# A two-layer graph-attention kernel: two PSUM banks of the first layer's tables serve the output products and the back-transposes once the tables are made

## The chip, the cores and the metric

The kernel runs on one core of a Trainium2 chip. The metric is the device time of one execution in microseconds (us). Three runs of the kernel before gave 2523.47, 2530.24 and 2531.26 us; the median, 2530.24, is the time to compare with. One further execution was taken with the hardware profiler; all traces here are of such an execution.

The names of the engines are those of the profile: PE is the matrix engine (PEld its weight loads), DVE the vector engine, ACT the scalar engine, POOL the engine that here mostly issues indirect DMAs, SP the engine that issues plain DMAs.

## The reference, cut to what matters

The input x has 8 batches of 2048 nodes with 256 features; adj is a sparse symmetric 0/1 matrix of 2048 x 2048, some 9 neighbours a node.

```python
def layer0(x):                               # 4 heads of 64
    q, k, v = x @ Wq.T + bq, x @ Wk.T + bk, x @ Wv.T + bv
    s = clip(q k^T / 8, -10, 10); s = where(adj == 0, -10, s)
    attn = softmax of s inside each chunk of 256 keys   # 8 softmaxes for a row
    out = x + (sum over the chunks of attn v) @ Wo.T + bo
    return layernorm(x + layernorm(out) * gamma + beta)
def layer1(x):                               # 4 heads of 64
    Wh = x @ W;  e = leaky_relu(Wh_i a_src + Wh_j a_dst), only where adj != 0
    return layernorm(x + elu(softmax(e) Wh))
```

The kernel doesn't compute the dense matrices. Each node has a list of its neighbours, and rows of keys and values are fetched by these lists.

## The kernel before

**Tiles and lists.** `edge_lists` makes neighbour lists and sorts the nodes by their number of neighbours, so that a tile of 128 nodes t needs a known number of slots, CAPS[t] (24 for tile 0, 5 for tile 15, 164 in all 16 tiles). Batches go in groups: layer 0 works on G = 2 batches at a time (4 groups g of 16 tiles, so 64 steps i = 0 to 63), layer 1 on 4 batches at a time (2 groups p of 16 tiles, so 32 steps).

**A step of layer 0.** `fetch0` gathers, with one indirect DMA a slot on POOL (line L489), rows of the table `kv_d[g]` into buffers `u`, two slots each; there are 14 of these buffers in a ring. `scores0` forms the scores on DVE (L547, L554) and PE (L566, L576), `softmax0` the weights, and `context0` weighs the gathered rows on DVE (L501) and ACT (L507) and sums them on PE into a bank `acc` (L514); ACT copies the sum out as `cT` (L626). Only when L514 has read a buffer `u` can POOL gather into it again. One step later `finish0` multiplies `cT` by Wo into a PSUM bank (L635, with the bias by L313), DVE reads that bank twice (L641), and then come the two layernorms on ACT and DVE (L451 to L470, L645, L647), whose result is `o`. Two steps later `rows1` transposes `o` (L307, ACT copy L658) and multiplies it by W, batch by batch, into a PSUM bank each (L663, copied out by L664 to L666); SP stores the rows into layer 1's table `wh_d` (L667).

**The tables.** While group g is worked on, `tables` makes the tables of group g + 1, one tile a step, in two banks named `tk` (`chunk_x` L336, keys and values L372 and L376, queries L385, and two small products in a group's last tile). The tables of the last group, 3, are finished in step 47.

**A step of layer 1.** `fetch1` gathers rows of `wh_d[p]` in the same ring; `softmax1` (L680 to L700) forms the weights, `context1` weighs and sums (L501, L507, L514) into two banks `acc`, which ACT copies out as two tiles `hT` (L722), and SP loads the residual `xr` (L725). One step later `finish1` transposes each `hT` back into a PSUM bank (L734), ACT takes the exponential from it (L737), DVE the maximum (L738), and then come L741, the layernorm, and, later still, scatters of the result on POOL (L748, L753).

**The eight PSUM banks** are two `acc`, two `tf`, one `pr`, two `tk` and one `mf`. In the loop, `mf` is used by `rows1` (two times a step of layer 0), `finish0` (once) and `finish1` (two times a step of layer 1); every use waits until the one before has been read out.

**The order.** `seq` lists the steps: 32 of layer 0, then two of layer 0 and one of layer 1 by turns, three steps of layer 1, and 16 of layer 1 alone. In one pass of the loop the calls stand in this order: scores0, the softmax1 of the next layer-1 step, finish1 and context1 of the one that waits, rows1(i-2), finish0(i-1), tables, softmax0, context0. That order is what a compiler reads: it places buffers, sets the semaphores and fixes each engine's own order of instructions, which isn't quite that of the text; on the chip each engine follows that order and waits where it must.

Of the kernel before, what the change touches and what calls it, by code (L numbers as in the profile page):

```python
# [36 lines left out]
G = 2  # L37
# [136 lines left out]
def sparse_path(ctx: ExitStack, tc: tile.TileContext, keep, x, adj, Wq, bq, Wk, bk, Wv, bv, Wo, bo, gamma, beta, W, a,  # L174
# [6 lines left out]
    NG = B // G  # L181
# [50 lines left out]
    def bank(tag, bufs=2):  # L232

        return ps.tile([P, 512], F32, tag=tag, name=tag, bufs=bufs)
# [75 lines left out]
    def add_bias(dst, bias):  # L310

        for c in range(KC):
            nc.tensor.matmul(dst[:, c * P:(c + 1) * P], bias[:, c:c + 1].to_broadcast([P, P]), ident,  # L313
                             is_transpose=True, start=False, stop=c == KC - 1, skip_group_check=True)
# [132 lines left out]
    def spread(src, sums, n):  # L447


        nm = small.tile([P, n], F32, tag=f"nm{n}", name="nm")  # L450
        nc.scalar.mul(nm, sums, -1.0 / F)  # L451
        m2 = small.tile([P, n], F32, tag=f"m2{n}", name="m2")
        for k in range(n):
            sq = small.tile([P, F], BF16, tag="sq", name="sq", bufs=1)
            nc.scalar.activation(sq, src[:, k, :], AF.Square, bias=nm[:, k:k + 1], accum_out=m2[:, k:k + 1])  # L455
        y = small.tile([P, n], F32, tag=f"y{n}", name="y")
        nc.scalar.activation(y, m2, AF.Ln, scale=1.0 / F, bias=eps)
        nc.scalar.activation(y, y, AF.Exp, scale=-0.5)
        r = small.tile([P, n], F32, tag=f"r{n}", name="r")
        nc.vector.scalar_tensor_tensor(r, m2, F * EPS, y, op0=ALU.add, op1=ALU.mult)  # L460
        nc.vector.scalar_tensor_tensor(r, r, -0.5 / F, y, op0=ALU.mult, op1=ALU.mult)
        nc.vector.scalar_tensor_tensor(r, r, 1.5, y, op0=ALU.add, op1=ALU.mult)
        return nm, r

    def normalized(dst, src, sums, n):

        nm, rs = spread(src, sums, n)
        nc.vector.tensor_tensor(nm, nm, rs, op=ALU.mult)
        for k in range(n):
            nc.scalar.activation(dst[:, k, :], src[:, k, :], AF.Identity, scale=rs[:, k:k + 1], bias=nm[:, k:k + 1])  # L470
# [44 lines left out]
                                 start=first and k == 0 and c == 0, stop=last and k == n - 1, skip_group_check=True)  # L515


    got0, st0 = {}, {}

    late = []  # L520
# [108 lines left out]
    def finish0(g, t):  # L629
        cT = st0.pop((g, t))  # L630
        xb = got0.pop((g, t))[0][:, GF:].rearrange("p (b f) -> p b f", b=G)
        po = bank("mf", 1).rearrange("p (b f) -> p b f", b=G)
        for b in range(G):
            for kc in range(KC):
                nc.tensor.matmul(po[:, b, :], cT[:, b * KC + kc, :], wo[:, kc, :], start=(b == 0 and kc == 0),  # L635
                                 stop=False, skip_group_check=True)
            add_bias(po[:, b, :], biasO[g][:, b])
        o = work.tile([P, G, F], F32, tag="o", name="o")
        sums = small.tile([P, 2, G], F32, tag="sums", name="sums")
        for b in range(G):  # L640
            nc.vector.tensor_tensor_reduce(out=o[:, b, :], in0=po[:, b, :], in1=xb[:, b, :], scale=1.0, scalar=0.0,  # L641
                                           op0=ALU.add, op1=ALU.add, accum_out=sums[:, 0, b:b + 1])
        nm, rs = spread(o, sums[:, 0], G)
        for b in range(G):
            nc.vector.scalar_tensor_tensor(o[:, b, :], o[:, b, :], nm[:, b:b + 1], gamma_r, op0=ALU.add, op1=ALU.mult)  # L645
        for b in range(G):
            nc.vector.scalar_tensor_tensor(o[:, b, :], o[:, b, :], rs[:, b:b + 1], xb[:, b, :], op0=ALU.mult, op1=ALU.add,  # L647
                                           accum_out=sums[:, 1, b:b + 1])
        normalized(o, o, sums[:, 1], G)
        nc.sync.dma_start(x1_d[g // 2][t * P:(t + 1) * P, g % 2, :].rearrange("p (b f) -> p b f", b=G), o)  # L650
        st0[g, t] = o
# [76 lines left out]
    def finish1(p, t):  # L728
        hTs, xr = st1.pop((p, t))
        sums = small.tile([P, 2 * G], F32, tag="sums1", name="sums1")  # L730
        for k, hT in enumerate(hTs):
            ph = bank("mf", 1)
            for c in range(G * KC):
                nc.tensor.transpose(ph[:, c * P:(c + 1) * P], hT[:, c, :], ident)  # L734

            ex = hT.rearrange("p c r -> p (c r)")
            nc.scalar.activation(ex, ph, AF.Exp)  # L737
            nc.vector.scalar_tensor_tensor(xr[:, k], ph, 0.0, xr[:, k], op0=ALU.max, op1=ALU.add)  # L738
            for b in range(G):
                xb, c = xr[:, k, b * F:(b + 1) * F], k * G + b  # L740
                nc.vector.scalar_tensor_tensor(xb, ex[:, b * F:(b + 1) * F], 1.0, xb, op0=ALU.min, op1=ALU.add,  # L741
                                               accum_out=sums[:, c:c + 1])
        yv = xr.rearrange("p k (b f) -> p (k b) f", f=F)
        normalized(yv, yv, sums, 2 * G)

        def scatter():
            if p < NG // 2 - 1:
                nc.gpsimd.indirect_dma_start(  # L748
                    out=hold_v[p][t], out_offset=bass.IndirectOffsetOnAxis(ap=node[:, t:t + 1], axis=0),
                    in_=xr.rearrange("p k f -> p (k f)"), in_offset=None)  # L750
                return
            for b in range(p * 2 * G, (p + 1) * 2 * G):
                nc.gpsimd.indirect_dma_start(  # L753
                    out=out_v[t * B + b],
                    out_offset=bass.IndirectOffsetOnAxis(ap=nodeb[:, t, b - p * 2 * G:b - p * 2 * G + 1], axis=0),
                    in_=yv[:, b - p * 2 * G, :], in_offset=None)
        late.append(scatter)
# [23 lines left out]
    def release(p, t):  # L781


        b0, rows = p * 2 * G, slice(t * P, (t + 1) * P)
        tc.keep_in_program_order(nc.sync.dma_start(
            out_v[NT * B + t * B + b0].rearrange("(b n) f -> n b f", b=B)[rows, b0:b0 + 2 * G, :],
            hold_d[p][rows, :].rearrange("n (b f) -> n b f", f=F)))

    def scatters():
        for f in late:  # L790
            f()
        late.clear()

    def at(i):
        return i // NT, order[i % NT]

    def at1(i):
        return i // NT, order[i % NT] if i >= NT else order1[i]
# [3 lines left out]
    def fetch(k):  # L802

        while fetched[0] <= min(k, len(seq) - 1):
            layer, i = seq[fetched[0]]
            (fetch1(*at1(i)) if layer else fetch0(*at(i)))
            fetched[0] += 1
# [3 lines left out]
    for k, (layer, i) in enumerate(seq):  # L811
        g, t = at1(i) if layer else at(i)
        between = layer == 0 and seq[k + 1][0] == 1
        tables_first = layer == 0 and seq[k + 1][0] == 0 and seq[k + 1][1] % NT == 0
        if not tables_first:
            fetch(k + 1)
        scatters()
        if layer == 0:
            scores0(g, t)
            if between and i + 1 < NG * NT:  # L820
                softmax1(*at1(seq[k + 1][1]))
            if waiting is not None:

                if waiting:
                    finish1(*at1(waiting - 1))
                context1(*at1(waiting))
                waiting = None
            if i > 1:
                rows1(*at(i - 2))
            if i:  # L830
                finish0(*at(i - 1))
            if g + 1 < NG:
                tables(g + 1, i % NT)
            if tables_first:
                fetch(k + 1)
            softmax0(g, t)
            context0(g, t)
        elif seq[k - 1][0] == 0 and seq[k - 1][1] + 1 < NG * NT:
            waiting = i
        else:  # L840

            last = seq[k - 1] == (0, NG * NT - 1)
            if last:
                rows1(*at(NG * NT - 2))
                finish0(*at(NG * NT - 1))
            softmax1(g, t)
            if last:
                rows1(*at(NG * NT - 1))
            finish1(*at1(i - 1))
            context1(g, t)  # L850
            if i >= NT + 2:
                release(g - 1, i - NT - 2)
    scatters()
    finish1(*at1(NG // 2 * NT - 1))
    scatters()
    for t in range(NT - 2, NT):
# [430 lines left out]
```

## Time and profile before

| what | value |
|---|---|
| median of three runs | 2530.24 us (2523.47 to 2531.26) |
| the profiled execution's own time | 2397.55 us |
| its span, first to last instruction | 2395.8 us |
| mean TensorE clock granted | 0.885 of full speed |
| PE, busy | 1900.4 us, 79% |
| PE weight loads, busy | 1622.0 us, 68% |
| DVE, busy | 1833.5 us, 77% |
| ACT, busy | 1409.0 us, 59% |
| POOL, busy | 1505.0 us, 63% |
| DMA, moved | 669.10 MB, mean 279 GB/s |
| L635 `finish0` products | 512 instructions, median 379 ns |
| L663 `rows1` products | 512 instructions, median 386 ns |
| L734 `finish1` transposes | 256 instructions, median 273 ns |

The shares are means over stages that differ. The last instruction that writes a `tk` bank starts at 1429.5 us; layer 0's last `finish0` products start at 1969.9 us; from there on only layer 1 runs. The profiled execution is 132.7 us shorter than the median of the timed runs.

### The profile page before, as it was taken

What the parts mean: (1) busy time and instruction counts of PE and PEld (TensorE: products, weight loads), DVE (VectorE), ACT (ScalarE), POOL (GpSimd) and SP (SyncE); (2) the same over time, 40 slices, a digit from 0 to 9 for tenths busy, and PEclk for the clock granted to TensorE, in tenths of its full rate; (3) what the DMA queues carried; (4) which work ended last, traced back from release to release, by engine and by line L of the source; (5) the groups of instructions that cost most, each with busy time, mean ns of one, the idle gap of its engine ahead of it and who ended that gap; (6) DMA issues with size and microseconds to landing.
All of it is one profiled execution on the core that took longest, in us unless ns stands there. A gap on an engine that the chain in (4) does not pass through costs nothing. (4 is left out here: it accounts for less than half of the span.)

```text
span 2395.8 us, 38844 instructions
## 1 busy us (share of the span) xinstructions
PE 1900.4 (79%) x11946; PEld 1622.0 (68%) x11946; DVE 1833.5 (77%) x4099; ACT 1409.0 (59%) x5036; POOL 1505.0 (63%) x1230
## 2 busy tenths in 40 slices
PE   7686889889899898999988885888678786664764
PEld 5565677778778787777876774776566675554653
DVE  6864587877588988588988886887788887775775
ACT  4573455546566555655565665664356677665766
POOL 3125455672666676376668856774677685787883
PEclk9897899899999999999998997987878987877887
DMA  7737877795889798598879977896679896786884
GB/s 259 242 137 272 265 270 281 260 346 209 316 287 320 260 334 319 212 388 298 302 258 353 360 281 238 285 321 221 230 274 326 306 319 248 278 310 231 302 296 154
DMA packets 239982, 669.10 MB, mean 279 GB/s; under 512 B 43688, under 2 KB 70059, under 8 KB 237719
## 3 DMA queue, kind: packets, MB, share of 16 engines
q0 software_dynamic: 156800, 505.01, 60.1%
q1 hardware_dynamic: 79248, 151.55, 17.2%
q10 hardware_dynamic: 3718, 9.97, 1.3%
q8 instruction: 98, 1.61, 0.3%
q14 instruction: 118, 0.96, 0.1%
HBM read 612.79 MB, written 126.36 MB: 309 GB/s over the span
## 5 line engine op out<-in xcount | busy, mean ns | idle before, releaser
L489 POOL DMA_INDIRECT u<-kv_d,idx x656 | 810.2, 1235 | 436.4 <-PE acc L514 185.7
L514 PE MATMUL acc<-ident,u 128*128 128x128 f32 x5248 | 713.4, 291 | 157.0 <-DVE u L501 89.0
L514 PEld LDWEIGHTS acc<-ident,u 128*128 128x128 f32 x5248 | 637.5, 151 | 220.7 <-DVE u L501 133.2
L489 POOL DMA_INDIRECT u<-wh_d,idx x328 | 416.5, 1270 | 148.2 <-issue 76.4
L566 PE MATMUL pr<-ident,u 128*128 128x128 f32 (+1 forms) x1984 | 287.0, 295 | 78.7 <-DVE u L547 77.2
L501 DVE TENSOR_TENSOR u<-u,al 128x1024 f32<-128x1024 f32 x280 | 334.5, 1234 | 1.5
L566 PEld LDWEIGHTS pr<-ident,u 128*128 128x128 f32 (+1 forms) x1984 | 245.4, 151 | 110.8 <-DVE u L547 104.6
L547 DVE TENSOR_TENSOR u<-u,qx 128x1024 f32<-128x1024 f32 (+1 forms) x248 | 302.0, 1218 | 18.3 <-DMA u<-kv_d,idx 15.1
L501 DVE TENSOR_TENSOR u<-u,z 128x1024 f32<-128x1024 f32 x266 | 314.4, 1212 | 0.6
L507 ACT ACTIVATE u<-u,z 128x64 f32<-128x64 f32 x1008 | 262.0, 337 | 25.0 <-DVE z L700 17.1
L507 ACT ACTIVATE u<-u,al 128x64 f32<-128x64 f32 x800 | 209.1, 342 | 23.2 <-DVE al L607 22.3
L663 PE MATMUL mf<-wa,x1T 128*128 128x264 f32 x512 | 167.6, 455 | 23.1 <-ACT x1T L658 14.8
L351 POOL TENSOR_TENSOR xt<-xt,beta_r 128x1024 f32<-128x1024 f32 x32 | 77.1, 2410 | 143.1 <-PE tk L336 126.3
L385 PE MATMUL tk<-wq,xT 128*128 128x256 f32 x512 | 145.2, 397 | 24.4 <-ACT kvs L379 24.4
L451 ACT ACTIVATE nm<-sums 128x2 f32<-128x2 f32 (+1 forms) x160 | 32.4, 202 | 221.3 <-DVE sums L641 122.6
L372 PE MATMUL tk<-wkv,xT 128*128 128x256 f32 x512 | 151.7, 410 | 12.9 <-ACT xC L341 12.6
L635 PE MATMUL mf<-wo,cT 128*128 128x256 f32 x512 | 148.4, 415 | 6.3 <-ACT whs L666 5.3
L376 PE MATMUL tk<-wkv,xC 128*128 128x256 f32 x512 | 144.5, 399 | 0.0
L663 PEld LDWEIGHTS mf<-wa,x1T 128*128 128x128 f32 x512 | 101.7, 218 | 59.7 <-ACT x1T L658 23.6
L455 ACT ACTIVATE sq<-o,nm 128x256 bf16<-128x256 f32 x256 | 129.7, 507 | 5.3
L554 DVE TENSOR_TENSOR u<-u,qx 128x1024 f32<-128x1024 f32 (+1 forms) x96 | 116.0, 1214 | 16.6 <-DMA qx<-qx_d,node 7.1
L590 DVE TENSOR_SCALAR sc<-tf 128x64 f32<-128x64 f32 (+5 forms) x64 | 14.0, 218 | 138.2 <-PE tf L576 138.2
(168 smaller groups left out, 3254.0 us busy)
## 6 DMA issues: line engine op xcount, KB each, us to landing
kv_d<-kvs SPq DMA_DIRECT2D x48, 512.0 KB, 6.0
wh_d<-whs SPq DMA_DIRECT2D x64, 260.0 KB, 5.8
xt<-in_x_dram SPq DMA_DIRECT2D x64, 256.0 KB, 4.8
qx_d<-xt SPq DMA_DIRECT2D x32, 512.0 KB, 4.4
qx_d<-qs SPq DMA_DIRECT2D x64, 256.0 KB, 5.8
x_d<-o SPq DMA_DIRECT2D x64, 256.0 KB, 5.2
xr<-x_d SPq DMA_DIRECT2D x32, 512.0 KB, 4.9
u<-kv_d,idx POOLq DMA_INDIRECT x656, 6.5
```

The lines of the kernel that those rows point to most:

```text
L372: nc.tensor.matmul(pm[:, 0:F], xT[:, b * KC + kc, rows], wkv[:, kc, 0:F], start=(kc == 0), stop=False, skip_group_check=True)
L376: nc.tensor.matmul(pm[:, F:], xC[:, b * KC + kc, rows], wkv[:, kc, F:], start=False, stop=(kc == KC - 1), skip_group_check=True)
L385: nc.tensor.matmul(qb, xT[:, b * KC + kc, rows], wq[:, kc, :], start=(b == 0 and kc == 0), stop=False, skip_group_check=True)
L455: nc.scalar.activation(sq, src[:, k, :], AF.Square, bias=nm[:, k:k + 1], accum_out=m2[:, k:k + 1])
L489: nc.gpsimd.indirect_dma_start(out=u[:, k, 0:width], out_offset=None, in_=table, in_offset=bass.IndirectOffsetOnAxis(ap=idx[:, t, s0 + k:s ...
L501: nc.vector.tensor_tensor(pv, pv, av, op=ALU.mult)
L507: nc.scalar.activation(pe, pe, AF.Copy, scale=al[:, e, s0 + k:s0 + k + 1])
L514: nc.tensor.matmul(acc[:, c, :], part[:, k, c * P:(c + 1) * P], ident, is_transpose=True, start=first and k == 0 and c == 0, stop=last and ...
L547: nc.vector.tensor_tensor(prod.rearrange("p k j (s w) -> p k j s w", w=W8), u[:, :, 0:GF].rearrange("p s (k j w) -> p k j s w", k=UNIT, w=W8),
L566: nc.tensor.matmul(pr[0:n * W8, k, :], prod[:, j // (NJ // UNIT), j % (NJ // UNIT), :], ident, is_transpose=True, start=(j == 0), stop=(j ...
L635: nc.tensor.matmul(po[:, b, :], cT[:, b * KC + kc, :], wo[:, kc, :], start=(b == 0 and kc == 0), stop=False, skip_group_check=True)
L663: nc.tensor.matmul(pw[:, 0:F + 2 * H], xT[:, b * KC + kc, :], wa[:, kc, :], start=(kc == 0), stop=(kc == KC - 1))
```

## The change

After the scores of each step of layer 0, a flag is set to whether the group at work is the last one (g = 3, steps 48 to 63). While it is not set, `finish0` and `finish1` take their bank from `mf`, as before. Once it is set, they take it from the two `tk` banks. `rows1` stays with `mf`. Nothing is added to or taken from what is computed.

```diff
+    made = [False]
+
+    def end_bank():
+        return bank("tk") if made[0] else bank("mf", 1)
...
     def finish0(g, t):
...
-        po = bank("mf", 1).rearrange("p (b f) -> p b f", b=G)
+        po = end_bank().rearrange("p (b f) -> p b f", b=G)
...
     def finish1(p, t):
...
-            ph = bank("mf", 1)
+            ph = end_bank()
...
             scores0(g, t)
+            made[0] = g + 1 == NG
```

The first user of a `tk` bank in its new role is `finish0` of step 47, which is called in step 48. In all, 17 calls of `finish0` (steps 47 to 63) and 28 calls of `finish1` (layer-1 steps 4 to 31; two banks each) change their bank.

## The prediction

> **What bounds the kernel now.** The change acts only after the tables are made, so I read the span by stages first: the busy time of each engine in four stretches. The columns are the stretch, its length, busy us and (instructions) of PE, its weight loads, DVE, ACT and POOL, the TensorE clock, the DMA share and GB/s.
>
> ```profile
> 1000.00:1430.00 430.00, 380.69 (x2518) 326.67 (x2519) 357.68 (x734) 261.57 (x970) 304.80 (x236) 0.96 0.89 325
> 1430.00:1700.00 270.00, 200.35 (x1256) 173.64 (x1255) 203.83 (x458) 153.04 (x562) 180.76 (x146) 0.80 0.79 272
> 1700.00:1990.00 290.00, 219.25 (x1390) 187.37 (x1388) 245.75 (x539) 172.35 (x637) 205.95 (x158) 0.85 0.81 284
> 1990.00:2200.00 210.00, 133.75 (x901) 116.14 (x900) 144.25 (x373) 144.10 (x502) 153.57 (x125) 0.80 0.74 270
> 2200.00:2396.00 196.00, 113.56 (x772) 96.64 (x772) 134.21 (x310) 126.89 (x448) 133.07 (x108) 0.79 0.69 249
> ```
>
> With the tables gone, no engine is full: from 1430 to 1990 DVE works 449.6 of 560 us, PE 419.6, POOL 386.7. But in POOL's timeline two indirect DMAs in a row always stand 0.30 us apart, so its 304 instructions occupy 386.7 + 304 x 0.30 = 478 us, 85% of this stage. From 1990 to 2396 the same sum is 286.6 + 233 x 0.30 = 357 of 406 us, and between 2063 and 2348 I find no gap of POOL above 1.5 us. POOL paces; what can be won is its gaps. Its waits from 1428 to 1990 (who waited, for whom, us in total, times, longest):
>
> ```profile
> POOL u L489 <- issue: 64.2, 186, 7.8
> POOL u L489 <- PE acc L514: 61.6, 27, 14.9
> POOL qx L527 <- DVE o L647: 8.5, 1, 8.5
> ```
>
> The "issue" line is mostly the 0.30 us spacing. The second counts: POOL can't gather because PE hasn't yet summed a buffer (L514). What PE did before its longest case shows in the timeline from 1634 to 1670 (start, us, engine and line; in brackets the idle time before it and what ended it):
>
> ```profile
> 1637.33 0.59 ACT L626 COPY cT<-acc 128x512 f32<-128x512 f32 x1 [2.71 <-PE acc L514]
> ...
> 1641.35 1.39 PE L566 MATMUL pr<-ident,u 128*128 128x128 f32 x8 [4.05 <-DVE u L547]
> ...
> 1646.35 1.09 ACT L470 ACTIVATE o<-o,nm,r 128x256 f32<-128x256 f32 x2 [4.12 <-DVE nm L468]
> ...
> 1654.34 2.13 PE L663 MATMUL mf<-wa,x1T 128*128 128x264 f32 x4 [0.59 <-ACT whs L666]
> ...
> 1657.06 2.07 PE L635 MATMUL mf<-wo,cT 128*128 128x256 f32 x4 [0.59 <-ACT whs L666]
> ...
> 1661.73 0.42 DVE L641 CUSTOM_DVE_ANT_0 o<-mf,qx 128x256 f32<-128x256 f32 x1 [3.82 <-PE mf L313]
> ...
> 1662.65 1.08 PE L734 MATMUL mf<-ident,hT 128*128 128x128 f32 x4 [0.96 <-DVE sums L641]
> ...
> 1663.70 6.51 PE L514 MATMUL acc<-ident,u 128*128 128x128 f32 x48
> ...
> 1665.94 1.79 POOL L489 DMA_INDIRECT u<-kv_d,idx  x1 [14.92 <-PE acc L514]
> ```
>
> finish0's input cT is there at 1637.9, PE is idle for 4.05 us, and mf is free (its last reader, L641 of the step before, ended at 1632.5). Yet L635 comes at 1657.1, behind both L663 of rows1, whose o was made only at 1647.4. It is so in every step of this stage: L635 follows its cT by 10 to 29 us (once 55), always behind the L663 pair, and rows1 stands before finish0 in the text. L734 of finish1(12) runs at 1991.0, 46 us after its hT (1944.3 to 1945.4), also behind rows1. PE itself does leave the text's order (L514 of context1(13) runs at 1957, before the L307 that the text has ahead of it). So I read: **a one-bank tag is handed out in the order of the text**, and a user that is ready waits for one that isn't. That is worse than the short waits between two users.
>
> **What the Trainium skill says.** "Perfetto Trace Analysis", section Optimization Strategy: look for the gaps of the contended engine, and the same gap repeating can mean that there isn't enough SBUF or PSUM for the next tile. POOL's gaps agree. "PSUM — Partial Sum Buffer", section on bank collisions: engines are to be kept apart by bank, so a reader blocks the writer of the next tile; here 0.59 us pass from ACT's reads to the next L663 or L635. "TensorE: Matmul & The Clock Gate", section on HAM oscillation: PE's idle gaps throttle its clock. The trace agrees in kind: four L663 take 1.16 us at 1965.25 and 2.13 us at 1654.34, and the clock is 0.96 in the tables' stage, 0.80 after it. Fewer instructions in a burst ahead of L514 are so worth between 1 and 2 times their fast price.
>
> **The change part by part.** Nothing is added or removed: 17 finish0 (12 PE instructions each) and 28 finish1 move from mf to two tk banks. No DMA and no arithmetic changes, so the edit itself costs nothing; it moves waits.
>
> (a) *finish0, from 1430 to 1970.* L635 and L313 no longer stand behind rows1; with cT there they fit PE's gaps. Then the PE burst in front of L514 is shorter by one finish0: 2.2 us at the fast clock (1947.56 to 1949.99, less what is woven in), 4.2 at the slow one (1657.06 to 1661.7), and 0.6 of waiting. Six long gaps of POOL end right behind such a burst, at 1633, 1666, 1705, 1789, 1867 and 1904 (9.48, 14.92, 7.53, 2.17, 5.01, 5.39 us). Three at the slow clock give 4.8, 6.8 (with L734 and its wait of 0.96) and 2.17 (all there is), three at the fast one 2.9 each: 22.5. The gap of 8.50 at 1741 waits for L647, which is finish0's own end: it goes when finish0 is early. A scatter's gap of 5.73 at 1483 waits for finish1. Together 36.7 us at most. Not all can stay: DVE has 110 us of idle in this stage, 32.0 of them L641 waiting for PE, and what POOL starts sooner meets the ring again. I take a third, **12 us**; bounds 0 and 37.
>
> (b) *The transition.* POOL's first gather of p = 1 needs every row of wh_d, so rows1(63), so finish0(63):
>
> ```profile
> 1951.59 0.56 ACT L626 COPY cT<-acc 128x512 f32<-128x512 f32 x1
> ...
> 1968.75 1.13 PE L635 MATMUL mf<-wo,cT 128*128 128x256 f32 x4
> ...
> 1990.98 1.11 PE L734 MATMUL mf<-ident,hT 128*128 128x128 f32 x4 [0.59 <-ACT whs L666]
> ...
> 1993.79 1.06 POOL L489 DMA_INDIRECT u<-wh_d,idx  x1 [12.39 <-issue]
> ```
>
> L635 could start at 1952.2, 16.6 us sooner. From L641 (1971.2) the chain takes 22.6 us to the gather; begun at about 1955 it ends near 1977, or later if rows1(62), whose o comes at 1963, or DVE's weighting is in the way. POOL has gathers of p = 0 to issue until 1981.4, so the gap of 12.39 us can close wholly. The next gap, 5.63 us at 2001.8, waits for L514 behind four L734 in a row that wait for L663 and for each other; it can close too. Bounds 0 and 18; I take **10**.
>
> (c) *Layer 1 alone.* The second L734 waits for L738 of the first (45.6 us of PE in 12 waits). But POOL is full there, so this is off the path, and I cost it at nothing: POOL's stream of gathers hides it; without that cover it would be some of DVE's 9.7 us of waiting for L737. Three gaps at 2029, 2046 and 2063 (3.17, 3.57, 3.68) wait for finish1 or the engine it shares: bounds 0 and 10.4, I take 2. At the very end L738 (2376.14) needn't wait for a second L734: L738 could follow its fellow at 2374.3, with the L741 behind it: **1 us**.
>
> Sum: 12 + 10 + 2 + 1 = 25 us of the profiled execution's 2397.55 (span 2395.8), so 2372.5. The timed median is 132.7 us above that execution, and no row says where; I carry the difference over unstretched: 2530.24 - 25 = **2505.2**.
>
> **Rivals.** *B, only the short waits go.* The compiler keeps finish0 behind rows1 for another reason than the bank, or POOL's gaps refill from another wait. Then what goes is PE's waiting for mf between users from 1428 to 1990: L635 4.3, L734 7.3 and 3.9, 15.5 us, of which a third on the path: 5 us, **2525**. For it: L514's gap at 1486.8 (14.00 us, for DVE) has nothing to do with mf. Against it: the free bank at 1637.
>
> *C, slower: early work gets in front on DVE.* Each engine's order is fixed beforehand. finish0's DVE block is 2 x 0.42 (L641), 2 x 0.52 (L645), 2 x 0.51 (L647), 6 accumulator reads or so at 0.08 and 6 small ones at 0.16: 4.4 us. Where it is now placed ahead of the products or the weighting that a buffer's release waits for, POOL waits 4.4 us more. From six of 16 steps on (26 us) that eats the gain; at nine (40 us) the kernel is slower by 15: **2545**. For it: DVE is 85% busy from 1700 to 1990. Against it: DVE waits for finish0's bank (32.0 us) now, and layer 1's own stage is POOL's.
>
> **How the numbers follow.** A gets 0.66, B 0.17, C 0.17. A alone reaches from 10 us to the bounds' sum of 66 us, of which I take 55: 2475 to 2520. The range must hold most of B and the near part of C: 2475 to 2540; outside lie the far end of C and a gain beyond 55. A measurement of this kernel tells about 0.3% (7.6 us) from no change. A and a little of B, less the weak end of A, are faster by more: 0.66; same 0.17; slower 0.17.
>
> **What would show it.** Step (a): L635 soon after its cT and often ahead of L307; "DVE o L641 <- PE mf" (under tk) well under 32 us; POOL's waits for L514 from 1428 to 1990 under 50 us. Step (b): POOL's gap before p = 1 under 5 us. Step (c): L734 pairs without a wait for L738, and layer 1 alone about as long as before, some 400 us. I'm wrong if L635 still trails rows1 (B), or if L635 is early and POOL's waits for L514 grow, with DVE's finish0 block ahead of L501 (C).

## The result, and the profile after

The changed kernel took 2553.84 us (median of 20 executions, 2528.09 to 2576.19), the kernel before on the same chip 2536.78 us (20 executions): a ratio of 1.0071, 95% interval 1.0044 to 1.0097. It is slower by 0.7%, where 1% less was forecast. Ratios here leave out executions more than 1.5% above the fastest one of their kernel, and so rest in places on few of them; beside them I give the difference of the means of all executions, with a 95% bound: here +18.2 ± 7.1 us. The profiled execution of the changed kernel took 2541.85 us (span 2540.0, mean TensorE clock 0.864). Lines of the code past 517 have moved by 6: L635 is now L641, L641 is L647, L663 is L669, L734 is L740, L748 is L754.

The stages first, as before (stretch, length, busy us and instructions of PE, PEld, DVE, ACT and POOL, clock, DMA share, GB/s). The first lies in the tables, the next two are layer 0's last group beside layer 1, the last two layer 1 alone:

```profile
1000.00:1500.00 500.00, 412.11 (x2654) 352.69 (x2655) 361.64 (x746) 272.38 (x1009) 286.80 (x232) 0.92 0.77 275
1553.00:1800.00 247.00, 178.20 (x1150) 154.44 (x1150) 191.83 (x445) 146.68 (x545) 156.45 (x130) 0.84 0.76 267
1800.00:2085.00 285.00, 200.26 (x1230) 170.35 (x1230) 211.91 (x452) 138.38 (x510) 178.17 (x142) 0.82 0.71 250
2110.00:2320.00 210.00, 129.27 (x864) 118.38 (x863) 146.26 (x358) 142.09 (x503) 152.50 (x124) 0.77 0.80 292
2320.00:2540.00 220.00, 128.21 (x877) 115.63 (x875) 147.00 (x340) 141.00 (x498) 150.22 (x118) 0.76 0.64 227
```

The tables' stage, which the change doesn't touch, is slower too: DMA moves 275 GB/s there against 325, DVE is busy 72% of it against 83%. So this trace and that of before differ by more than the change, and I keep that for the experiments. POOL's waits while both layers run, 1553 to 2085:

```profile
POOL u L489 <- PE acc L514: 95.1, 22, 13.8
POOL u L489 <- issue: 58.2, 183, 2.5
POOL hold_d L754 <- ACT xr L470: 16.7, 1, 16.7
```

The forecast wanted the first under 50 us (61.6 before). The wait of 8.5 us for the end of finish0 is gone, but a scatter (L754) waits 16.7 us. The transition, where layer 0 ends:

```profile
2084.73 0.59 ACT L632 COPY cT<-acc 128x512 f32<-128x512 f32 x1 [2.98 <-remote]
...
2085.37 1.68 PE L641 MATMUL tk<-wo,cT 128*128 128x256 f32 x4 [2.99 <-issue]
...
2099.27 0.38 DVE L706 TENSOR_TENSOR z<-z,r 128x224 f32<-128x224 f32 x1
2099.69 1.22 DVE L501 TENSOR_TENSOR u<-u,z 128x1024 f32<-128x1024 f32 x1
...
2104.92 1.94 POOL L489 DMA_INDIRECT u<-wh_d,idx  x1 [12.59 <-PE acc L514]
```

L641 starts 0.05 us after cT is done, where L635 took 16.6 us. It is so in all 17 steps: L641 follows cT by 0.05 to 4.4 us, against 9.8 to 54.6 us before. The reading of the bank's order was right. But POOL has a new gap of 12.59 us. DVE did finish0(63)'s and finish1(12)'s L647 to L653, L744 and L747 between 2089.52 and 2099.05, inside softmax1(13)'s chain (L690 at 2090.46, L706 at 2099.27); only then comes the weighting L501 that POOL's next buffer waits for. That is rival C's mechanism, seen here at one place.

### The profile page after: what moved, and what is told of

Its sections match the earlier page's. It is cut to its first block, busy times and chain, and to the rows that moved or that the text cites. A ratio compares the mean times of both kernels' runs of the same rounds, so it can differ in the third digit from the quotient of the medians.

```text
span 2540.0 us, 38839 instructions
## 1 busy us (share of the span) xinstructions
PE 1925.9 (76%) x11946; PEld 1653.5 (65%) x11946; DVE 1829.7 (72%) x4099; ACT 1408.9 (55%) x5036; POOL 1478.5 (58%) x1230
## 4 chain that ended last, share of the span: by engine, by line
PE 28%; DVE 16%; issue 9%; ACT 8%; DMA 5%; another core or an unknown queue 3%; POOL 1%; SPq 0%; POOLq 0%; DVEq 0%; ACTq 0%
PE acc L514 10%; DVE u L501 6%; PE pr L572 4%; PE mf L669 4%; ACT u L507 2%; DVE u L553 2%; DMA u<-wh_d,idx 2%; ACT sq L455 2%; PE mf L641 2%; PE tf L582 2%; DMA u<-kv_d,idx 1%; PE tk L641 1%; PE tk L376 1%; PE tk L385 1%
## 5 line engine op out<-in xcount | busy, mean ns | idle before, releaser
L489 POOL DMA_INDIRECT u<-kv_d,idx x656 | 793.4, 1209 | 551.3 <-PE acc L514 280.1
L514 PE MATMUL acc<-ident,u 128*128 128x128 f32 x5248 | 721.6, 296 | 177.8 <-issue 106.3
L514 PEld LDWEIGHTS acc<-ident,u 128*128 128x128 f32 x5248 | 659.2, 154 | 232.8 <-issue 127.1
L489 POOL DMA_INDIRECT u<-wh_d,idx x328 | 402.3, 1227 | 184.5 <-issue 81.9
L501 DVE TENSOR_TENSOR u<-u,al 128x1024 f32<-128x1024 f32 x280 | 336.9, 1243 | 1.4
L501 DVE TENSOR_TENSOR u<-u,z 128x1024 f32<-128x1024 f32 x266 | 313.2, 1213 | 0.4
L553 DVE TENSOR_TENSOR u<-u,qx 128x1024 f32<-128x1024 f32 (+1 forms) x248 | 296.4, 1195 | 18.4 <-DMA u<-kv_d,idx 16.6
L669 PE MATMUL mf<-wa,x1T 128*128 128x264 f32 x512 | 168.6, 456 | 52.2 <-issue 25.5
L385 PE MATMUL tk<-wq,xT 128*128 128x256 f32 x512 | 157.3, 423 | 46.5 <-ACT kvs L379 39.4
L669 PEld LDWEIGHTS mf<-wa,x1T 128*128 128x128 f32 x512 | 101.0, 217 | 91.7 <-issue 35.6
L385 PEld LDWEIGHTS tk<-wq,xT 128*128 128x128 f32 x512 | 98.3, 213 | 60.8 <-ACT kvs L379 43.7
L372 PEld LDWEIGHTS tk<-wkv,xT 128*128 128x128 f32 x512 | 95.9, 206 | 59.2 <-ACT kvs L379 29.7
L378 ACT COPY kvs<-tk 128x256 f32<-128x256 f32 x128 | 47.5, 371 | 138.2 <-remote 71.3
```

What stands on the lines that cost most here:

```text
L372: nc.tensor.matmul(pm[:, 0:F], xT[:, b * KC + kc, rows], wkv[:, kc, 0:F], start=(kc == 0), stop=False, skip_group_check=True)
L385: nc.tensor.matmul(qb, xT[:, b * KC + kc, rows], wq[:, kc, :], start=(b == 0 and kc == 0), stop=False, skip_group_check=True)
L489: nc.gpsimd.indirect_dma_start(out=u[:, k, 0:width], out_offset=None, in_=table, in_offset=bass.IndirectOffsetOnAxis(ap=idx[:, t, s0 + k:s ...
L501: nc.vector.tensor_tensor(pv, pv, av, op=ALU.mult)
L514: nc.tensor.matmul(acc[:, c, :], part[:, k, c * P:(c + 1) * P], ident, is_transpose=True, start=first and k == 0 and c == 0, stop=last and ...
L553: nc.vector.tensor_tensor(prod.rearrange("p k j (s w) -> p k j s w", w=W8), u[:, :, 0:GF].rearrange("p s (k j w) -> p k j s w", k=UNIT, w=W8),
```

## The experiments

**First, the halves.** The theories were: (1) finish0's early vector-engine blocks stand in front of the weighting (rival C), (2) finish1 and its scatters do, (3) any new order moves the time by some tenths of a per cent. Kernel before on this chip: 2589.27 us.

`control` is the kernel before with blank lines added, the same program.

> The kernel before with seven empty lines, so that its lines carry the numbers of the changed kernel. The same program: ratio 1.000, and its spread says what a ratio is worth. Its trace is the one to compare with. Theory 1 (finish0's early layernorm gets in front of the weighting): POOL's waits for L514 between the end of the tables and the end of layer 0 are near 60 us here, against 107.7 in the changed kernel. Rival 2 (the chip of the first trace was a faster one, and the waits of any kernel are longer on this one): they are near 100 here too.

Measured: 0.9974 (0.9940 to 1.0007), mean +1.7 ± 7.1 us. So large is the uncertainty of one comparison. POOL's wait for L514 from the end of the tables to the end of layer 0 (1608 to 2147):

```profile
POOL u L489 <- PE acc L514: 120.0, 27, 16.6
```

That isn't near 60 us, as in the first trace; it is more than the changed kernel's 95.1. Two more traces that have the old order in this stage and such a chip, `before_shift` and `l1part` (below), show 79.2 and 113.5 us for it. So the rise from 61.6 to 95.1 us isn't the change's: the rival of a quicker chip holds.

`f0only` leaves finish1 on mf:

```diff
-            ph = end_bank()
+            ph = bank("mf", 1)
```

> Only finish0 takes the tk banks, finish1 stays with mf. Theory 1 (finish0 starts 10 to 29 us sooner and its layernorm gets in front of what the sums L514 wait for): the whole loss, ratio 1.007. Rival 2 (finish1's early start does it, its scatters stand in POOL's order ahead of gathers and wait): ratio 1.000. Rival 3 (any new order of instructions gives or takes some tenths of a per cent, whoever is moved): anything from 0.993 to 1.010.

Measured: 1.0003 (0.9973 to 1.0033), mean -0.9 ± 6.3 us.

`f1only` leaves finish0 on mf:

```diff
-        po = end_bank().rearrange("p (b f) -> p b f", b=G)
+        po = bank("mf", 1).rearrange("p (b f) -> p b f", b=G)
```

> Only finish1 takes the tk banks, finish0 stays with mf behind rows1. Theory 1: 1.000 or a little below, 0.998. Rival 2 (finish1's early start does it): 1.007. Rival 3 (any new order): anything from 0.993 to 1.010, and not what the other half leaves over.

Measured: 0.9995 (0.9966 to 1.0024), but mean +8.6 ± 7.2 us.

`onequeue` gives `rows1` the same banks, so that all three stand in one line for two of them:

```diff
-            pw = bank("mf", 1)
+            pw = end_bank()
```

> rows1 takes the tk banks as well once the tables are made, so that all three users share one line of two banks in the order of the text, and finish0 stays behind rows1. The second bank without the overtaking. Theory 1: the loss is gone, ratio 0.995 to 1.000. Rival 2 (finish1): finish1 is behind rows1 as well, so the loss is gone too; the runs with one half tell the two apart. Rival 3: anything from 0.993 to 1.010.

Measured: 0.9993 (0.9963 to 1.0024), mean -4.3 ± 7.4 us. Here L641 stayed 9.8 to 49.1 us behind cT (in the repetition below): the second bank alone does not free finish0, the order of the text does bind. Theory 1 as stated fell: finish0 alone costs nothing that can be measured, though in the trace of `f0only` L641 follows cT by less than 5 us.

**Second, the stages.** Kernel before: 2580.95 us. `both2` is the changed kernel again.

> The change as it is, once more, beside its parts on one chip. Theory 1 (finish0's and finish1's vector-engine blocks, both early now, stand ahead of the softmax and the weighting while layer 0 and layer 1 run by turns): 1.007. Theory 2 (the loss is made where layer 0 ends and in layer 1 alone: the blocks of finish0(63) and finish1(12) inside softmax1(13)'s chain, and finish1's pairs after that): 1.007. Theory 3 (the loss is an offset of a few tenths of a per cent that any new order or any chip gives): anything from 0.998 to 1.004.

Measured: 1.0052 (1.0022 to 1.0082), mean +15.3 ± 7.4 us. The loss is repeated; with the first result +16.8 ± 5.1 us.

`l0part` goes back to mf at each pass of layer 1 alone; `l1part` has `True` in that place, and leaves out the line that sets the flag in layer 0:

```diff
             last = seq[k - 1] == (0, NG * NT - 1)
+            made[0] = False
```

> finish0 and finish1 use the tk banks only while layer 0 runs (steps 48 to 63); finish0(63) and all of layer 1 alone are back on mf. Theory 1: 1.006, and POOL's waits for L514 over 100 us in the stage of both layers as in the changed kernel. Theory 2: 1.000, with the gap of about 12 us before p = 1 back and the first gathers after it without a long wait for L514. Theory 3: 0.997 to 1.004.

Measured: 1.0028 (1.0000 to 1.0055), mean +13.2 ± 8.6 us.

> The tk banks only from the first pass of layer 1 alone: finish0(63) and finish1(12) to finish1(31) on tk, all before on mf. Theory 1: 1.000, with the order of the stage of both layers as before. Theory 2: 1.005, with the gap before p = 1 gone and a wait of about 12 us of POOL for L514 in its place, as in the changed kernel. Theory 3: 0.997 to 1.004.

Measured: 0.9998 (0.9956 to 1.0040), mean +7.7 ± 8.3 us. Most of the loss seems to lie where both layers run; for the rest these two don't decide.

`held` cuts finish0 in two once the tables are made, with its vector part (`norms0`, L647 to the store) behind the weighting in the text:

```diff
             context0(g, t)
+            if made[0] and i:
+                norms0(*at(i - 1))
```

> The whole change, but finish0 is cut in two once the tables are made: its products stay where they are, and its vector-engine part (L647 to the store) is called after context0, so that it comes after the weighting in the text. finish1 stays early. Theory 1: much of the loss goes, 1.000 to 1.003, POOL's waits for L514 in the stage of both layers back to what the kernel before has on this chip. Theory 2: 1.007, since finish0(63) and layer 1 are not touched. Theory 3: 0.997 to 1.004.

Measured: 1.0101 (1.0059 to 1.0143), mean +19.7 ± 11.7 us. This says less than was wanted. In DVE's own order, as the trace shows it, the edit moved little: of 17 steps the last vector instruction of finish0 that makes `o` (L653 of the changed kernel) comes 1 to 5 weightings (L501) later than in the changed kernel in eight, and no later in the others; in the kernel before it is 1 to 21 later in fourteen. So `held` doesn't test whether later blocks help.

**Third, one scatter, and another chip.** In POOL's fixed order one instruction had moved far: the scatter of finish1(8) stands behind gather 688 of the changed kernel, `both2`, `l0part` and `held`, and behind gather 721 of the kernel before, `f0only`, `f1only` and `onequeue`. In the first four kernels POOL waits 14.7 to 16.7 us in front of it. `scat_back`, `l0_back` and `held_back` put it back in the changed kernel, `l0part` and `held` (`got[0]` is the last gather of a step):

```diff
+        pin[p, t] = got[0]
...
-                nc.gpsimd.indirect_dma_start(
+                with tc.issue_after(pin[at1(10)].ins) if (p, t) == at1(8) else nullcontext():
+                    nc.gpsimd.indirect_dma_start(
```

> The change as it is, beside three kernels in which one scatter is put back. New theory 4: one scatter of layer 1, that of finish1(8), stands 33 gathers earlier in POOL's fixed order than in the kernel before, and POOL stands 14 to 17 us in front of it with those gathers queued behind: 1.005 to 1.007 again, with one wait of POOL L754 for L470 of about 15 us. Theory 1 (the vector engine's early blocks in front of the weighting): 1.005 to 1.007 too.

> The whole change, with one ordering edge more: the scatter of finish1(8) is issued after the gathers of layer 1's step 10, where it stands in the kernel before. Theory 4: the long wait of L754 is gone and with it the loss, 0.998 to 1.002. Theory 1: 1.005 to 1.007, since the vector engine's order in front of the weighting stays nearly what it is. If the forecast gain was there and only hidden by that scatter: 0.990 to 0.995.

> The tk banks only while layer 0 runs (as in the run with that part alone, which lost 13 us in the mean) with the same edge for the scatter of finish1(8). Theory 4: 0.998 to 1.002. Theory 1: 1.003 to 1.006. If the forecast gain of the stage of both layers was hidden by that scatter: 0.993 to 0.996.

> The whole change with finish0's vector-engine part called after context0 (1.010 without the edge) and the same edge for the scatter of finish1(8). Theory 4: some 15 us less than without the edge, 1.001 to 1.005. Theory 1: still 1.006 to 1.010.

Measured, against a kernel before of **2390.29 us** on this chip:

| kernel | ratio (95% interval) | mean, us |
|---|---|---|
| `both3`, the change | 0.9911 (0.9884 to 0.9939) | -21.7 ± 5.5 |
| `scat_back` | 0.9935 (0.9907 to 0.9962) | -14.8 ± 5.1 |
| `l0_back` | 0.9954 (0.9928 to 0.9980) | -11.7 ± 5.3 |
| `held_back` | 0.9944 (0.9920 to 0.9967) | -15.0 ± 5.3 |

The theories for `both3` had no gain: **on this chip the change gains 22 us, close to the 25 forecast.** The time of the kernel before is near that of the trace the forecast was read from (2397.55 us). POOL's waits in `both3` while both layers run (1442 to 1918), and the transition:

```profile
POOL u L489 <- PE acc L514: 37.3, 20, 8.7
POOL hold_d L754 <- ACT xr L470: 13.8, 1, 13.8
```

```profile
1935.38 1.93 POOL L489 DMA_INDIRECT u<-wh_d,idx  x1 [7.28 <-PE acc L514]
```

The wait for L514 is under the 50 us asked for; the scatter waits 13.8 us here too, and putting it back gains nothing: the mean of `scat_back` is 6.9 ± 6.0 us above that of `both3`.

**What differs between the chips.** `control` and the kernel before are one program, so their traces can be laid over each other. ACT's largest waits in `control` with the releaser "remote", one that the trace doesn't find on this core:

```profile
ACT prT L578 <- remote: 56.6, 12, 9.5
ACT kvs L378 <- remote: 54.2, 10, 15.5
ACT hT L728 <- remote: 45.7, 11, 9.2
```

`control` has 60 such waits on ACT, 234 us in all; the changed kernel's first profile 53 with 184 us; all fifteen traces with spans from 2519.7 to 2610.1 us (I call them the slow traces) have 36 to 71. The five traces of 2358 to 2396 us, the quick ones, have none. All but one of the ACT instructions that wait so in `control` read what PE wrote, so I call these waits late PE results.

One of them, in `control` and then in the kernel before:

```profile
426.74 1.09 PE L572 MATMUL pr<-ident,u 128*128 128x128 f32 x8
...
432.51 0.58 ACT L578 COPY prT<-pr 128x512 f32<-128x512 f32 x1 [7.19 <-remote]
```

```profile
419.43 1.04 PE L566 MATMUL pr<-ident,u 128*128 128x128 f32 x8
...
420.50 0.59 ACT L572 COPY prT<-pr 128x512 f32<-128x512 f32 x1 [2.59 <-PE pr L566]
```

The transposes end at 427.83 and 420.47; the copy starts 4.68 us after them in `control`, 0.03 us in the kernel before. PE's ends are modelled in a profile, so it can't be told whether the products or the signal of their end came late. Some places recur: at this one `control`, `l1part` and `both2`, on two chips, wait 7.19, 7.20 and 7.21 us, and all slow traces 5.0 to 8.1 us. At the L378 that comes 1004.5 us into the quick trace the three wait 15.46, 13.97 and 13.96 us, all slow traces 8.3 to 15.5, and the quick trace 0.0. But by no means all do: of the late results over 2 us in the fifteen slow traces, 43% lie on 21 instructions that are so late in eight or more of them, and 12% on instructions that are so late in one alone.

`control` and the kernel before drift apart by these jumps: ACT's instructions are 12.5 us later in `control` near 493 us, 75.9 near 1015, 141.8 near 1559 and 213.5 near 2571. At the 60 waits the lag grows by 213.2 us in all; everything between them adds up to nothing.

**Fourth, do the late results explain the sign?** Two theories were left: (4) the scatter costs on such chips, (5) late results sit at fixed places of PE's stream, and a new order puts them on worse instructions. The two shift kernels run 48 more transposes at PE's start:

```diff
+        pd = bank("mf", 1)
+        for _ in range(48):
+            nc.tensor.transpose(pd[:, 0:P], ident, ident)
```

> The kernel before with 48 transposes of the identity into an unused bank at PE's very start, where PE has nothing to do; the later order is that of the kernel before. Theory 5 (stalls at fixed places of PE's stream, so their place in the program moves with it): on a chip with the remote waits these sit on other instructions than before, and the time differs by any amount from 0.993 to 1.007, not by what 48 transposes cost (under 7 us, and PE is idle there). Theory 4: 0.998 to 1.002, and the remote waits stay on their instructions. On a chip without remote waits: 0.998 to 1.002 for both.

> The changed kernel with the same 48 transposes. Theory 5: on a chip with remote waits they sit on other instructions than in the changed kernel, and the ratio is no longer 1.005 to 1.007: anything from 0.992 to 1.010. Theory 4: 1.005 to 1.007, since POOL's order is unchanged. On a chip without remote waits: 0.989 to 0.994, as the change alone.

> The changed kernel with the scatter of finish1(8) back behind the gathers of layer 1's step 10, once more. On a chip with remote waits, theory 4: 0.998 to 1.001, some 15 us less than the changed kernel. Theory 5: 1.003 to 1.010, as the changed kernel or by chance otherwise. On a chip without remote waits: 0.991 to 0.996, as in the run before.

Measured (kernel before 2539.59 us): `before_shift` 1.0007 (0.9979 to 1.0035), mean -0.3 ± 6.4 us; `after_shift` 1.0046 (1.0022 to 1.0071), +12.1 ± 5.8 us; `scat_back2` 0.9995 (0.9953 to 1.0036), but that ratio hangs on one short execution (2506.76 us), its median is 8.0 us above and its mean +12.3 ± 7.1 us. The 48 transposes take 8.2 us. In `before_shift` the copy above still waits 5.82 us, at 435.44, and 20 of its 28 late results over 2 us are on instructions that are late in `control` too. So theory 5 fell in its form, that a shift of PE's stream moves them. In `scat_back2` every scatter from 1553 us to cT of step 63 waits 0.31 us at most. Its ratio says that the loss is gone, its mean that it is there: theory 4 stays undecided on such chips.

**Fifth, the halves again.** Kernel before 2582.56 us, the chip of the first halves again.

> finish0 alone on the tk banks. On a chip with many remote waits: 0.998 to 1.002, as before. On one without: if the gain is made by finish0 no longer waiting for rows1, as step (a) and the first half of step (b) forecast, 0.992 to 0.995; if it needs both halves, 0.998 to 1.002.

> finish1 alone on the tk banks. On a chip with many remote waits: 1.001 to 1.005. On one without: 0.997 to 1.000 if step (a) is right, since finish0 and with it rows1 stay where they were; under 0.995 if the gain is finish1's.

> All three users on the two tk banks, handed out in the order of the text: one bank more, but finish0 stays behind rows1. On a chip with many remote waits: 0.996 to 1.002. On one without: 0.997 to 1.000 if the order is what makes the gain, 0.990 to 0.994 if it is the second bank alone.

Measured: `f0only2` 0.9999 (0.9966 to 1.0032), mean -2.8 ± 7.2 us; `f1only2` 1.0104 (1.0042 to 1.0165), +13.0 ± 11.9 us, from 6 executions (about ± 14 with the small number allowed for); `onequeue2` 0.9976 (0.9945 to 1.0007), -4.3 ± 8.0 us. The means weighted with those of the first halves: finish0 alone -1.7 ± 4.7 us, finish1 alone +9.8 ± 6.2 us, one queue -4.3 ± 5.4 us. So on such chips the half that costs is finish1's, if either: its first ratio (0.9995) doesn't show a loss, its second does. No kernel here was measurably faster than the kernel before on a chip with late results.

## Why the prediction was wrong

**The step that failed** is the last line of the sum: "The timed median is 132.7 us above that execution, and no row says where; I carry the difference over unstretched." The trace was of an execution without late PE results. The timed ones are at the level of the slow traces, and the one of the changed kernel that was traced among them has 53. The difference was no constant to add: it is made of waits all along the program, and where they are the change loses 17 us, where they aren't it gains 22. That the late results themselves take the gain away is argued, not shown: one quick chip stands against at least three slow ones, and no kernel here adds late results or takes them away.

**The reading of the bank** was right on both kinds of chip: L641 comes 0.05 to 5.6 us after cT in `both3`, 0.05 to 4.4 us in the first profile after. Two details were misread. The 0.59 us given for the time from ACT's reads to the next product is PE's idle time between two products; L663 at 1654.34 starts 0.06 us after the last of ACT's three reads ends. And of the six long gaps that at 1789 (2.17 us) does not end right behind a burst of finish0: PE did eight transposes of L566 and waited 1.13 us for DVE in between.

**Step (a)**, 12 us forecast with bounds of 0 and 37, came on the quick chip. `l0_back`, which has the change in this stage alone and the scatter put back, gains 11.7 ± 5.3 us. POOL's waits for L514 fell from 61.6 to 37.3 us and the wait of 8.5 us went, against a scatter's wait that rose from 5.7 to 13.8; DVE's wait for finish0's bank fell from 32.0 to 16.5 us (in `both3`, 1442 to 1935).

In quick traces the time from cT of step 47 to cT of step 63 was 503.5 us in the kernel before and 476.5, 484.5, 487.4 and 485.9 in the four kernels with the change there, a mean of 20 us less. But the stretch ahead of it, where nothing is changed, was 1448.1 us before and 1440.2 in the mean of the four, so about 8 us of such a difference can be chance.

The TensorE clock in that stage was 0.83 before and 0.86 to 0.89 in the four, and PE's idle gaps over 2 us were 19 before and 11 to 13 in the four. That agrees in kind with what the Trainium skill says in "TensorE: Matmul & The Clock Gate", section on HAM oscillation, that idle gaps of PE throttle its clock; but PE's idle time in all stayed (125.7 us, then 119.6 to 130.7), and no run varies the gaps alone.

In the slow traces nothing of the 20 us is left. Single traces scatter there: 512.7 to 541.3 us with the old order (`before_shift`, `control`, `l1part`, mean 531.0), 524.5 to 547.6 with the change (the first profile, `both2`, `l0part`, `held`, `after_shift`, `scat_back2`, mean 535.1).

**Steps (b) and (c)**, 13 us forecast: in quick traces from cT of step 63 to the end, 444.3 us before, 439.9, 441.0 and 440.3 with the change there, some 4 us less. The gap of 12.39 us did go, as forecast, but a wait for L514 came in its place, 7.28 us there and 12.59 us on the first chip. Step (b)'s chain had "or later if ... DVE's weighting is in the way"; it was the other way round, the weighting stood behind the early blocks. In layer 1 alone PE's 45.6 us of waits between the two back-transposes are gone in `both3`, and the stage is hardly shorter, which fits that they were costed at nothing. That 22 us came where 25 were forecast is then partly luck, since most of these 13 us did not come.

**Rival C** had the price (2545 us) and the sign, and its mechanism is seen in the transition. As the cause of the loss where both layers run, it fell in the form that was written, with finish0's 4.4 us block: `f0only` has these blocks where the changed kernel has them, within 3 weightings, and loses nothing. Nor did POOL's waits for L514 grow, once traces with late results are compared with each other.

**What stays open:** what costs the 17 us on chips with late results, and whether it is finish1's half. In `f1only` DVE's fixed order has fewer weightings (L501) ahead of finish1's L744: for three steps in a row 285, 295 and 311 instead of 294, 309 and 317, so its blocks come 6 to 14 weightings sooner, in front of work that a late PE result has already delayed. But the changed kernel has 290, 300 and 317 there, and `f0only`, which loses nothing, 289, 302 and 317. So this place in the order doesn't tell the kernels that lose from one that doesn't, and a kernel that holds finish1 back wasn't tried. The loss may also lie in the late results themselves. Span and sum of the late results mostly rise together (correlation 0.93 over the fifteen slow traces): on one chip `before_shift` has 140 us of them in 2519.7 us, `scat_back2` 188 in 2543.6, `after_shift` 177 in 2555.8, and span less sum is 2351 to 2380 us in all fifteen slow traces, with the old order and the new. Traces of single executions can't tell whether the change adds to the sum. Nor do the runs show why PE's results come late.

## What to carry to other kernels

Here a tag (the name that buffers share) with one buffer, and one with two as well (`onequeue`), served its users in the order of the text; compare when an input is ready with when it is used, step by step, and count the time lost there apart from short waits. Before a gain is summed up from one trace, ask whether that trace is an execution like those that are timed: a gap of 5% between the two needn't be a constant to carry over; here it was other waits, and with them the sign of a small gain was different. And a step that is made early starts more than itself: look on every engine at what it now stands in front of.

## What the runs showed of the hardware that was not expected

The same program took 2390 us on one chip and 2537 to 2589 us in the other measurements, on at least three chips. Between the traces of `control` and of the kernel before, the difference is made of 60 discrete delays of PE's results to ACT, of up to 15.5 us (up to 21.3 in other traces). Some 20 instructions are late in most of the slow traces, others in one alone, and 48 instructions more at the head of PE's stream left both the recurring places and the time as they were. The busy times of the engines hardly differ (PE 1900.4 us in the kernel before and 1955.5 in `control`, DVE 1833.5 and 1830.0 us). Only one chip was quick, and it was measured once, so that this is a property of the chip isn't shown.
